# A two-layer graph kernel: node counts from the comparison instruction, and a new order of the head

## The chip, the cores and the metric

The kernel runs on one core of a Trainium2 chip. The metric is the device time of one execution in microseconds, given as the median over several runs. Every number below comes from those runs or from one profiled execution of the same kernel.

The engines are named as in the profile: PE is TensorE (PEld its loading of weights), DVE is VectorE, ACT is ScalarE, POOL is GpSimd. SP issues most of the DMA transfers, and its own entries carry a q (SPq).

## The reference

For each of N = 128 graphs there are C = 128 nodes with D = 512 features (x, fp32), and a 128 x 128 matrix adj of weights, many of them zero.

```python
H  = (adj != 0)                       # incidence: node c lies in hyperedge e
w  = adj[:, 0, :]                     # first row: the hyperedges' weights
Dn = 1 / sum_e H[c, e] * w[e]         # 0 where the sum is not positive
Be = 1 / sum_c H[c, e]                # one over the number of nodes of a hyperedge
hypergraph_conv(x, W, b) = Dn * (H @ (Be * (H.T @ (x @ W.T)))) + b

# layer 0
h = relu(layernorm(x))
r = layernorm(relu(hypergraph_conv(h, W1, b1))) * gamma + beta    # 512 -> 1024
x = x + h + hypergraph_conv(r, W2, b2)                            # 1024 -> 512
# layer 1
h   = relu(layernorm(x))
agg = (adj @ h) / max(sum_j adj[i, j], 1e-6)
x   = x + relu(concat(h, agg) @ W.T)                              # 1024 -> 512
```

All of it is fp32. W1, W2 and W are the same for all graphs.

## The kernel before

One graph fills the 128 partitions, so the work goes graph by graph. [...]each large product is made of three: both operands are split into a high part h and a low part l, with a third part d made from the two. `product` sums h x h and l x l in one PSUM bank ("main") and d x d in a second, four or eight 128x512 matmuls for each part. The weights are split once, in the head: `Half.high` (ScalarE), `Half.low` and `Half.rest` (VectorE), each on one half of a weight tile at a time (index 0 or 1). The activations are split per graph: `conv1_high/low/rest` (z), `inner_high/low/rest` (n), `layer1_high/low/rest` (h, "layer 1's first operand"), `layer1_mean_high/low/rest` (b). In the profile w10h is the high part of the first half of W1, w31d the third part of the second half of W (w3), and so on; rm and rd are the two banks of the first convolution's product, gm and gd of the second's, bm/bd and am/ad of layer 1's two.

The stages of a graph, with the tiles that the text speaks of:

- `load_adjb` and `load_adj` fetch adj, once in 32x32 blocks (four transfers, adjb) and once as it is; `load_x` fetches x.
- `x_sums`, `x_spread`, `scales`, `x_norm`: the layer norm of x. ScalarE makes the two sums, VectorE the scales (lines 234 and 235, tile st), ScalarE the result h (line 239).
- `incidence` (VectorE, lines 290 to 299): transposes adj, compares with zero, counts the nodes of each hyperedge (cnt), and makes sb, the incidence divided by the count, with a further column of weights.
- `node_matrix`: TensorE makes S = H Be H.T and the sums for Dn from sb in one fp32 matmul (ps_s, line 305); ScalarE copies it to s. `node_scale` (VectorE, lines 315 to 319) makes Dn out of it.
- `conv1_nodes`: S is applied to h ahead of W1 (pz, line 343). `conv1_weights`: the product with W1, in two halves. `conv1_main` (ScalarE), `conv1_out` and `conv1_bias` put together r.
- `inner_sums`, `inner_spread`, `inner_norm`, `inner_out`, `inner_in`, `inner_turn`: relu and layer norm of r, then a way through DRAM (n_scratch, then nb) and a 32x32 transpose (nt), since the next product needs r with its features on the partitions.
- `conv2_weights`, `conv2_main`, `conv2_weights_out`, `conv2_bias`, `conv2_nodes`, `conv2_out`: second convolution; S is applied behind the weights here (py, line 517). `residual` adds h and b2 to x (GpSimd).
- `layer1_*`: layer norm, the same way through DRAM (h_scratch, hb, ht), product with both halves of W. `mean_operator`, `mean_out`, `mean_in`, `mean_transpose` make adj divided by its row sums, transposed and split (anp). `aggregate` multiplies it into the second half's product, three matmuls, the third of which needs the part bd (line 475).

In the head `beta_row(k)` multiplies the raw W2 by beta on TensorE (pc, line 185), and `scale_w2(k)` then scales that block of W2 by gamma; only after it can the block be split.

The order on each engine is written out by hand: `tc.manual_schedule()` keeps the program's order, so an instruction stands in its engine's queue where the program calls it, and waits there for its inputs. `head()` is a list of stages for the first graphs; then `step(s)` runs for s from -4 to 126, each with stages of five graphs in one fixed order; then `tail()`. `stage` keeps a set of what was done, so a step leaves out what the head did already. DMA issues stand in SP's queue in the program's order too, and each uses one of eight semaphores in turn, so it also waits for the transfer issued eight before it.

Of the kernel before, what the change touches and what calls it, by code (L numbers as in the profile page):

```python
# [24 lines left out]
def gnn_kernel(  # L25
# [31 lines left out]
    nc = tc.nc  # L57
# [124 lines left out]
    def beta_row(k):  # L182
        if not BETA:
            BETA.append(bank("pc"))
        nc.tensor.matmul(BETA[0], vector_of(0, k).to_broadcast([P, P]), w2[k // KD].raw[:, k % KD],
                         start=(k == 0), stop=(k == KH - 1))
# [15 lines left out]
    @stage  # L202
    def load_x(g):
        X[g] = pool.tile([P, D], FP, tag="x", name="x_t", bufs=6)
        nc.sync.dma_start(out=X[g], in_=x[g])
# [6 lines left out]
    @stage  # L212
    def load_adjb(g, queue=nc.sync):
        ADJB[g] = pool.tile([P, P], FP, tag="adjb", name="adjb", bufs=2)
        load_blocks(ADJB[g], adj[g], queue)
# [15 lines left out]
    @stage  # L231
    def scales(g, kind):
        t = STATS[kind, g]
        nc.vector.reciprocal(t[:, 4:5], t[:, 3:4])  # L234
        nc.vector.tensor_tensor(t[:, 5:6], t[:, 1:2], t[:, 4:5], MUL)  # L235
# [49 lines left out]
    @stage  # L285
    def incidence(g):


        HT[g] = at = pool.tile([P, P], FP, tag="ht", name="adjt")
        nc.vector.transpose(at, ADJB.pop(g))  # L290
        SB[g] = sb = pool.tile([P, P + 1], FP, tag="sb", name="sb")
        nc.vector.tensor_scalar(sb[:, P : P + 1], at[:, 0:1], DOWN_12, None, MUL)
        nc.vector.tensor_scalar(at, at, 0.0, None, ALU.not_equal)
        cnt = pool.tile([P, 1], FP, tag="cnt", name="cnt", bufs=2)
        nc.vector.tensor_reduce(cnt, at, AX.X, ADD)

        nc.vector.tensor_scalar(cnt, cnt, 1.0, None, MAX)
        nc.vector.reciprocal(cnt, cnt)
        nc.vector.tensor_scalar(sb[:, :P], at, cnt, None, MUL)
# [26 lines left out]
    @stage  # L326
    def x_spread(g):
        spread((1, g), X[g], H0[g], D)

    @stage  # L330
    def x_norm(g):
        normalise((1, g), H0[g], X[g], AF.Relu)
# [63 lines left out]
    @stage  # L396
    def conv1_weights(g, half):
        PR[g, half] = product(Z[g], w1[half : half + 1], lambda pm: PY.update({(g, half): pm}), "r")

    @stage  # L400
    def conv1_main(g, half):
        if half == 0:
            R[g] = pool.tile([P, DH], FP, tag="r", name="r")
        copy(R[g][:, HALVES[half]], PY.pop((g, half)), AF.Copy, scale=DN[g][:, 1:2])  # L404
# [6 lines left out]
    @stage  # L411
    def conv1_bias(g, half, eng=nc.gpsimd):
        r = R[g][:, HALVES[half]]
        combine(eng, r, r, b1_bc[:, HALVES[half]], ADD)
# [268 lines left out]
    def head():  # L683
        copy(eps_root, eps, AF.Sqrt)
        load_x(0)
        load_adjb(2)
        for half in range(2):
            for i in range(2):
                load_w1(half, i)
        load_affine()  # L690
        load_adjb(0, nc.scalar)
        load_x(1)
        load_adjb(1)
        x_sums(0)
        load_adj(0)
        x_spread(0)
        for half in range(2):
            load_w2(half)
        load_bias(b2_bc, b2)
        w1[0].high(0)  # L700
        scales(0, 1)
        x_norm(0)
        w1[0].high(1)
        incidence(0)
        load_x(2)
        w1[0].low(0)
        node_matrix(0)
        conv1_nodes(0)
        w1[0].low(1)
        w1[1].high(0)  # L710
        w1[0].rest(0)
        conv1_high(0)
        w1[1].high(1)
        load_bias(b1_bc, b1)
        conv1_low(0)
        conv1_rest(0)
        incidence(1)
        x_sums(1, "A")
        x_spread(1)
        node_scale(0)  # L720
        w1[0].rest(1)
        scales(1, 1)
        w1[1].low(1)
        x_norm(1)
        conv1_weights(0, 0)
        beta_row(0)
        scale_w2(0, nc.scalar)
        conv1_main(0, 0)
        beta_row(1)
        scale_w2(1, nc.scalar)  # L730
        w1[1].low(0)
        w1[1].rest(0)
        w1[1].rest(1)
        node_matrix(1)
        node_scale(1)
        conv1_nodes(1)
        conv1_high(1, True)
        conv1_weights(0, 1)
        conv1_low(1)
        conv1_rest(1)  # L740
        beta_row(2)
        beta_row(3)
        conv1_main(0, 1)
        conv1_weights(1, 0)
        conv1_out(0, 0)
        scale_w2(2, nc.vector)
        scale_w2(3, nc.vector)
        conv1_bias(0, 0, nc.vector)
        w2[0].high(0)
        w2[0].high(1)  # L750
        conv1_out(0, 1)
        conv1_bias(0, 1, nc.vector)
        beta_row(4)
        beta_row(5)
        load_adjb(3)
        load_w3(0)
        load_w3(1)
        beta_row(6)
        beta_row(7)
        inner_sums(0)  # L760
        conv1_weights(1, 1)
        inner_spread(0)
        w2[0].low(1)
        residual(0)
        scale_w2(4, nc.vector)
        scale_w2(5, nc.vector)
        scales(0, 2)
        inner_norm(0)
        scale_w2(6, nc.vector)
        scale_w2(7, nc.vector)  # L770
        w2[0].low(0)
        incidence(2)
        inner_out(0)
        x_sums(2)
        x_spread(2)
        scales(2, 1)
        w2[1].high(0)
        w2[1].low(0)
        x_norm(2)
        node_matrix(2)  # L780
        w2[1].high(1)
        node_scale(2)
        load_adjb(4)
        conv1_nodes(2)
        conv1_main(1, 0)
        conv1_main(1, 1)
        conv1_high(2)
        w2[0].rest(1)
        conv1_low(2)
        conv1_rest(2)  # L790
        beta_out()
        inner_in(0)
        load_x(3)
        inner_turn(0)
        residual(1)
        conv1_out(1, 0)
        w3[0].high(0)
        conv1_bias(1, 0, nc.vector)
        w2[1].low(1)
        load_x(4)  # L800
        inner_high(0)
        conv1_weights(2, 0)
        conv1_out(1, 1)
        conv1_bias(1, 1, nc.vector)
        conv1_weights(2, 1)
        inner_low(0, nc.vector)
        w2[0].rest(0)
        inner_sums(1)
        inner_spread(1)
        w2[1].rest(0)  # L810
        scales(1, 2)
        inner_norm(1)
        inner_out(1)
        load_adjb(5)
        inner_rest(0)
        w3[0].high(1)
        w2[1].rest(1)
        incidence(3)
        conv2_weights(0)
        x_sums(3)  # L820
        x_spread(3)
        node_matrix(3)
        scales(3, 1)
        x_norm(3)
        residual(2)
        node_scale(3)
        conv2_main(0)
        conv1_main(2, 0)
        conv2_weights_out(0)
        conv1_nodes(3)  # L830
        conv2_bias(0, nc.vector)
        conv2_nodes(0)
        conv1_high(3, True)
        conv1_main(2, 1)
        conv1_low(3)
        conv1_rest(3)
        conv1_weights(3, 0)
        conv2_out(0)
        conv1_out(2, 0)
        conv1_bias(2, 0, nc.vector)  # L840
        layer1_sums(0)
        layer1_spread(0)
        inner_in(1)
        inner_turn(1)
        conv1_out(2, 1)
        conv1_bias(2, 1, nc.vector)
        inner_high(1)
        scales(0, 3)
        inner_low(1, nc.vector)
        inner_rest(1)  # L850
        layer1_norm(0)
        layer1_trip_out(0)
        w3[1].high(0)
        conv2_weights(1)
        inner_sums(2)
        inner_spread(2)
        w3[0].low(1)
        scales(2, 2)
        conv2_main(1)
        inner_norm(2)  # L860
        conv2_weights_out(1)
        mean_operator(0)
        conv2_bias(1, nc.vector)
        inner_out(2)
        conv2_nodes(1)
        conv1_weights(3, 1)
        w3[1].low(0)
        mean_out(0)
        w3[0].low(0)
        conv2_out(1)  # L870
        layer1_trip_in(0)
        w3[1].high(1)
        mean_in(0)
        load_adj(1)
        x_sums(4)
        residual(3)
        x_spread(4)
        scales(4, 1)
        x_norm(4)
        incidence(4)  # L880
        layer1_turn(0)
        w3[1].low(1)
        layer1_high(0)
        node_matrix(4)
        mean_transpose(0)
        node_scale(4)
        layer1_low(0, nc.vector)
        inner_in(2)
        w3[0].rest(1)
        w3[1].rest(1)  # L890
        w3[1].rest(0)
        w3[0].rest(0)
        load_x(5)
        layer1_rest(0)
        load_adjb(6)

    def tail():
# [182 lines left out]
```

## Time and profile before

| | |
|---|---|
| median of 5 runs | 2514.6 us (2514.28 to 2516.56) |
| the profiled execution | 2515.8 us, span 2514.0 us |
| mean granted TensorE clock | 0.994 |
| instructions in the profile | 41377 |
| PE busy in 260 to 1300 us | 1039.02 of 1040 us |

The span is the time from the first to the last instruction of the program. A line of the time line gives start, length, engine, source line, operation, output and inputs, the number of instructions merged into it, and in brackets the idle time of the engine ahead of it and what ended that. All starts are microseconds from the start of the span.

### The profile page before, as it was taken

Reading aid. Unit: us, or ns where it says so; the run is one execution under the profiler, and the core shown is the slowest. Engines: PE = TensorE matmul, PEld = TensorE weight load, DVE = VectorE, ACT = ScalarE, POOL = GpSimd, SP = SyncE. Lnnn points to the kernel's source line nnn. Section 1 sums busy time; section 2 is a strip of 40 time slices with the busy share of each in tenths; the row PEclk is TensorE's granted clock in tenths of the full one; section 3 lists DMA queues with packets and bytes.
Section 4 is the critical chain, followed back from the end, with each engine's and each line's share of the span. In section 5 each row is a group of like instructions: output and inputs, shape, how many; then the busy total and the mean of one; then the engine's idle time right before and its main releaser. Section 6 shows DMA issues by size and latency. Waiting matters only on the chain. (4 is left out here: it accounts for less than half of the span.)

```text
span 2514.0 us, 41377 instructions
## 1 busy us (share of the span) xinstructions
PE 2470.1 (98%) x11152; PEld 2004.4 (80%) x11152; DVE 2122.1 (84%) x4907; ACT 1977.7 (79%) x4112; POOL 1739.6 (69%) x2290
## 2 busy tenths in 40 slices
PE   6899999999999999999999999999999999999997
PEld 4688887888888888888888888888888888888885
DVE  7988888888888888888888888888888888888885
ACT  6787787778778878878887887887888788788874
POOL 2477677677767767777776776777677667767763
PEclk9899999999999999999999999999999999999999
DMA  6343344344344434333343443443444344344332
GB/s 175 95 127 121 125 126 122 122 127 128 119 126 127 125 121 133 120 123 126 124 125 126 127 121 122 130 126 120 125 127 125 120 133 121 120 128 129 120 120 83
DMA packets 409674, 311.90 MB, mean 124 GB/s; under 512 B 176736, under 2 KB 340576, under 8 KB 409440
## 3 DMA queue, kind: packets, MB, share of 16 engines
q1 hardware_dynamic: 408608, 309.18, 39.8%
q8 instruction: 88, 1.44, 0.2%
q14 instruction: 146, 1.20, 0.2%
q10 hardware_dynamic: 576, 0.07, 0.0%
q0 software_dynamic: 256, 0.01, 0.0%
HBM read 166.47 MB, written 142.61 MB: 123 GB/s over the span
## 5 line engine op out<-in xcount | busy, mean ns | idle before, releaser
L80 POOL TENSOR_TENSOR g<-g,c 128x256 f32<-128x256 f32 x252 | 181.4, 743 | 524.1 <-DVE g L508 400.4
L80 POOL TENSOR_TENSOR r<-r,b_bc 128x256 f32<-128x256 f32 x500 | 356.7, 744 | 20.6 <-DVE st L234 11.6
L80 POOL TENSOR_TENSOR nl<-nt,nh 128x256 fp32r<-128x256 f32 x504 | 358.2, 747 | 5.0 <-ACT nh L466 5.0
L80 POOL TENSOR_TENSOR hl<-ht,hh 128x256 fp32r<-128x256 f32 x254 | 180.9, 734 | 147.0 <-ACT hh L466 147.0
L80 POOL TENSOR_TENSOR x_t<-x_t,h 128x256 f32<-128x256 f32 x256 | 240.4, 962 | 47.0 <-ACT h L239 47.0
L80 POOL TENSOR_TENSOR bl<-gb_t,bh 128x256 fp32r<-128x256 f32 x256 | 260.2, 1040 | 9.7 <-PE am L385 9.7
L504 ACT ACTIVATE g<-gm 128x512 f32<-128x512 f32 x128 | 76.4, 597 | 212.9 <-PE gm L385 212.7
L239 ACT ACTIVATE h<-x_t,st 128x512 f32<-128x512 f32 x256 | 207.8, 812 | 35.2 <-DVE st L235 23.2
L475 DVE SCALAR_TENSOR_TENSOR nd<-nh,nl 128x1024 fp32r<-128x1024 f32 x128 | 208.1, 1626 | 25.2 <-POOL nl L80 25.2
L445 DVE STREAM_TRANSPOSE nt<-nb 128x1024 f32<-128x1024 f32 x128 | 159.4, 1245 | 61.1 <-DMA nb<-n_scratch 59.6
L223 ACT ACTIVATE h<-x_t 128x512 f32<-128x512 f32 x256 | 160.2, 626 | 60.7 <-DVE x_t L521 58.6
L80 POOL TENSOR_TENSOR x_t<-x_t,b_bc 128x256 f32<-128x256 f32 x256 | 184.8, 742 | 14.0 <-DMA b_bc<-in_b_dram 14.0
L385 PE MATMUL rm<-w11h,z 128*128 128x512 f32 x512 | 190.5, 494 | 0.0
L228 ACT ACTIVATE h<-x_t,st 128x512 f32<-128x512 f32 x256 | 184.7, 722 | 4.3
L409 DVE SCALAR_TENSOR_TENSOR r<-rd,dinv,r 128x512 f32<-128x512 f32 x256 | 186.3, 728 | 0.9 <-ACT r L404 0.6
L404 ACT ACTIVATE r<-rm,dinv 128x512 f32<-128x512 f32 x256 | 171.4, 670 | 3.1 <-DMA n_scratch<-r 1.4
L239 ACT ACTIVATE r<-r,st 128x1024 f32<-128x1024 f32 x128 | 158.0, 1234 | 1.7 <-DVE st L235 1.5
L385 PEld LDWEIGHTS rm<-w11h,z 128*128 128x128 f32 x512 | 96.6, 189 | 72.0 <-issue 60.2
L385 PE MATMUL bm<-w30h,hh 128*128 128x512 f32 x512 | 150.3, 415 | 3.3 <-ACT hh L466 3.3
L466 ACT ACTIVATE nh<-nt 128x1024 fp32r<-128x1024 f32 x128 | 135.2, 1056 | 19.3 <-DVE nt L445 18.6
L343 PEld LDWEIGHTS pz<-s,h 128*128 128x128 f32 x1024 | 134.3, 192 | 14.9 <-ACT s L307 4.0
L605 DVE SCALAR_TENSOR_TENSOR o<-ad,o 128x512 f32<-128x512 f32 x128 | 88.5, 692 | 68.1 <-ACT o L593 67.2
(127 smaller groups left out, 7251.7 us busy)
## 6 DMA issues: line engine op xcount, KB each, us to landing
n_scratch<-r SPq DMA_DIRECT2D x128, 512.0 KB, 2.6
nb<-n_scratch SPq DMA_DIRECT2D x512, 128.0 KB, 2.8
x_t<-in_x_dram SPq DMA_DIRECT2D x128, 256.0 KB, 2.8
h_scratch<-h SPq DMA_DIRECT2D x128, 256.0 KB, 2.1
hb<-h_scratch SPq DMA_DIRECT2D x512, 64.0 KB, 2.0
out_dram<-o SPq DMA_DIRECT2D x128, 256.0 KB, 2.8
adj_t<-in_adj_dram SPq DMA_DIRECT2D x128, 64.0 KB, 1.8
an_scratch<-adj_t SPq DMA_DIRECT2D x128, 64.0 KB, 2.6
```

The source lines that it names most:

```text
L80: eng.tensor_tensor(dst[:, s], a[:, s], b[:, s], op)
L223: copy(junk, src, func, accum_out=t[:, 0:1])
L228: copy(junk, src, AF.Square, bias=t[:, 1:2], accum_out=t[:, 2:3])
L239: copy(dst, src, func, bias=t[:, 5:6], scale=t[:, 4:5])
L343: nc.tensor.matmul(z[:, k * P : (k + 1) * P], H0[g][:, k * P : (k + 1) * P], S[g], start=True, stop=True)
L385: nc.tensor.matmul(pm, left[i](k), right(i, k), start=(i == 0 and k == 0), stop=(i == 1 and k == kk - 1))
L404: copy(R[g][:, HALVES[half]], PY.pop((g, half)), AF.Copy, scale=DN[g][:, 1:2])
L409: nc.vector.scalar_tensor_tensor(r, PR.pop((g, half)), dn[:, 0:1], r, MUL, ADD)
L445: nc.vector.transpose(nt.rearrange("p k (i b) -> p k i b", b=B), t.rearrange("p i k a -> p k i a"))
L466: copy(h, a, AF.Copy, scale=DOWN)
L475: nc.vector.scalar_tensor_tensor(t, h, 2.0**-12, low, MUL, SUB)
L605: nc.vector.scalar_tensor_tensor(o, pd, 4096.0, o, MUL, ADD)
```

## The change

Two things are changed. In `incidence`, which runs for each of the 128 graphs, the comparison with zero also sums its results along the row and writes the sum to cnt; the separate sum is gone. And in `head()` stages stand in another order; the stages themselves, `step` and `tail` are as before. In the last part of the head, layer 1's first operand for graph 0 (`layer1_low`, `layer1_rest`) is made ahead of the third parts of W's second half.

```diff
@@ incidence
-        nc.vector.tensor_scalar(at, at, 0.0, None, ALU.not_equal)
         cnt = pool.tile([P, 1], FP, tag="cnt", name="cnt", bufs=2)
-        nc.vector.tensor_reduce(cnt, at, AX.X, ADD)
+        nc.vector.tensor_scalar(at, at, 0.0, None, ALU.not_equal, ADD, accum_out=cnt)
@@ head
         load_adjb(0, nc.scalar)
+        load_adjb(1)
         load_x(1)
-        load_adjb(1)
         x_sums(0)
         load_adj(0)
         x_spread(0)
+        scales(0, 1)
...
         w1[0].high(0)
-        scales(0, 1)
+        load_x(2)
+        w1[0].high(1)
         x_norm(0)
-        w1[0].high(1)
         incidence(0)
-        load_x(2)
...
         conv1_rest(0)
-        incidence(1)
         x_sums(1, "A")
...
         w1[1].low(1)
         x_norm(1)
+        incidence(1)
         conv1_weights(0, 0)
+        conv1_main(0, 0)
         beta_row(0)
         scale_w2(0, nc.scalar)
-        conv1_main(0, 0)
+        node_matrix(1)
         beta_row(1)
+        w1[1].low(0)
         scale_w2(1, nc.scalar)
-        w1[1].low(0)
         w1[1].rest(0)
         w1[1].rest(1)
-        node_matrix(1)
-        node_scale(1)
         conv1_nodes(1)
...
         conv1_main(0, 1)
-        conv1_weights(1, 0)
+        w2[0].high(0)
         conv1_out(0, 0)
         scale_w2(2, nc.vector)
+        load_adjb(3)
         scale_w2(3, nc.vector)
+        conv1_weights(1, 0)
         conv1_bias(0, 0, nc.vector)
-        w2[0].high(0)
         w2[0].high(1)
         conv1_out(0, 1)
         conv1_bias(0, 1, nc.vector)
         beta_row(4)
+        load_w3(1)
+        load_w3(0)
         beta_row(5)
-        load_adjb(3)
-        load_w3(0)
-        load_w3(1)
         beta_row(6)
+        node_scale(1)
+        residual(0)
         beta_row(7)
         inner_sums(0)
         conv1_weights(1, 1)
+        w2[0].low(1)
         inner_spread(0)
-        w2[0].low(1)
-        residual(0)
         scale_w2(4, nc.vector)
         scale_w2(5, nc.vector)
         scales(0, 2)
-        inner_norm(0)
         scale_w2(6, nc.vector)
+        x_sums(2)
         scale_w2(7, nc.vector)
         w2[0].low(0)
         incidence(2)
+        inner_norm(0)
         inner_out(0)
-        x_sums(2)
         x_spread(2)
...
         w2[1].low(0)
+        node_matrix(2)
         x_norm(2)
-        node_matrix(2)
+        node_scale(2)
         w2[1].high(1)
-        node_scale(2)
...
         inner_in(0)
-        load_x(3)
         inner_turn(0)
         residual(1)
         conv1_out(1, 0)
         w3[0].high(0)
-        conv1_bias(1, 0, nc.vector)
+        load_x(3)
+        conv1_out(1, 1)
         w2[1].low(1)
         load_x(4)
+        conv1_bias(1, 0, nc.vector)
         inner_high(0)
         conv1_weights(2, 0)
-        conv1_out(1, 1)
         conv1_bias(1, 1, nc.vector)
...
-        load_adjb(5)
         inner_rest(0)
         w3[0].high(1)
+        load_adjb(5)
...
         conv1_high(3, True)
+        conv1_low(3)
         conv1_main(2, 1)
-        conv1_low(3)
...
         layer1_norm(0)
-        layer1_trip_out(0)
         w3[1].high(0)
         conv2_weights(1)
+        layer1_trip_out(0)
+        mean_operator(0)
         inner_sums(2)
...
         conv2_weights_out(1)
-        mean_operator(0)
         conv2_bias(1, nc.vector)
         inner_out(2)
+        mean_out(0)
+        w3[1].low(0)
         conv2_nodes(1)
+        w3[0].low(0)
         conv1_weights(3, 1)
-        w3[1].low(0)
-        mean_out(0)
-        w3[0].low(0)
-        conv2_out(1)
         layer1_trip_in(0)
         w3[1].high(1)
         mean_in(0)
         load_adj(1)
+        residual(3)
         x_sums(4)
-        residual(3)
...
         incidence(4)
+        conv2_out(1)
         layer1_turn(0)
...
         node_scale(4)
+        inner_in(2)
+        w3[0].rest(0)
         layer1_low(0, nc.vector)
-        inner_in(2)
         w3[0].rest(1)
+        layer1_rest(0)
+        w3[1].rest(0)
         w3[1].rest(1)
-        w3[1].rest(0)
-        w3[0].rest(0)
         load_x(5)
-        layer1_rest(0)
         load_adjb(6)
```

## The prediction

> **What bounds the kernel now.** I read the page first, then busy time by stretches, then the time line of the first 100 us engine by engine, last the DMA landings.
>
> ```profile
> PE 2470.1 (98%) x11152; PEld 2004.4 (80%) x11152; DVE 2122.1 (84%) x4907; ACT 1977.7 (79%) x4112; POOL 1739.6 (69%) x2290
> ```
> ```profile
> 0.00:20.00 20.00, 8.09 (x23) 5.90 (x24) 11.52 (x30) 11.36 (x22) 6.09 (x14) 1.00 0.77 217
> ...
> 60.00:80.00 20.00, 16.69 (x52) 11.73 (x52) 17.09 (x32) 14.36 (x28) 2.52 (x4) 0.76 0.23 77
> 80.00:100.00 20.00, 15.37 (x59) 11.88 (x58) 19.26 (x38) 11.71 (x27) 11.75 (x14) 0.81 0.23 65
> 100.00:120.00 20.00, 20.00 (x92) 16.34 (x92) 17.83 (x42) 16.23 (x33) 13.11 (x18) 1.00 0.43 130
> ...
> 1300.00:2350.00 1050.00, 1049.84 (x4789) 856.72 (x4788) 900.35 (x2092) 844.16 (x1766) 756.00 (x992) 1.00 0.40 125
> ```
>
> The first line is busy time by engine; the others give start and length of a stretch, busy us of TensorE, weight loads, VectorE, ScalarE and GpSimd, then the granted clock, DMA share and GB/s. From 100 us on TensorE is never idle (1049.84 of 1050), at the full clock, 19.07 us per graph. There a faster VectorE is worth nothing. All of TensorE's loss lies in the first 95 us (some 27 us idle, and a lower clock in four places) and in the last 64, which the change doesn't touch. So the change is worth what it moves the moment from which TensorE runs without a pause. These lines carry the head:
>
> ```profile
> 10.62 0.80 PE L305 MATMUL ps_s<-sb,adjt 128*128 128x129 f32 x2 [10.62 <-DVE sb L299]
> ...
> 23.18 1.16 PE L343 MATMUL pz<-s,h 128*128 128x128 f32 x8 [1.09 <-ACT s L307]
> ...
> 38.92 0.49 PE L305 MATMUL ps_s<-sb,adjt 128*128 128x129 f32 x2 [1.18 <-DVE sb L299]
> ...
> 54.78 1.20 PE L389 MATMUL gd<-w20d,nd 128*128 128x512 f32 x4 [0.86 <-DVE nd L475]
> ...
> 75.94 1.10 PE L517 MATMUL py<-g,s 128*128 128x512 f32 x2 [2.43 <-DVE g L80]
> ...
> 89.48 2.07 PE L389 MATMUL bd<-w30d,hd 128*128 128x512 f32 x4 [3.93 <-DVE hd L475]
> ```
> ```profile
> 8.80 0.23 DVE L293 TENSOR_SCALAR adjt<-adjt 128x128 f32<-128x128 f32 x1
> 9.06 0.29 DVE L295 TENSOR_REDUCE cnt<-adjt 128x1 f32<-128x128 f32 x1
> ...
> 34.87 0.17 DVE L234 RECIPROCAL st<-st 128x1 f32<-128x1 f32 x1 [1.08 <-ACT st L229]
> ...
> 73.60 0.69 DVE L508 TENSOR_TENSOR g<-gd,g 128x512 f32<-128x512 f32 x1 [0.29 <-PE gd L389]
> 74.21 0.27 DVE L249 TENSOR_REDUCE deg<-adj_t 128x1 f32<-128x128 f32 x1
> ...
> 85.34 2.35 DVE L136 TENSOR_TENSOR w31d<-w31l,w31h 128x1024 fp32r<-128x1024 f32 x2
> 87.61 1.21 DVE L136 TENSOR_TENSOR w30d<-w30l,w30h 128x1024 fp32r<-128x1024 f32 x1
> 88.75 0.68 DVE L475 SCALAR_TENSOR_TENSOR hd<-hh,hl 128x512 fp32r<-128x512 f32 x1
> ...
> 100.57 0.69 DVE L475 SCALAR_TENSOR_TENSOR bd<-bh,bl 128x512 fp32r<-128x512 f32 x1
> ```
>
> Each bracket is idle time and what ended it. VectorE is the late one. Three things are to be seen: g waits at 74.21 behind four mean_operator instructions; hd waits behind the weights' parts w31d; and at 34.87 VectorE itself waits for ScalarE's statistics.
>
> **The comparison.** Removed per graph: comparison and sum, 0.58 us from start to start (8.80 to 9.38). In their place is one comparison that also sums. No row shows that form. The nearest rows: the sum alone 0.286 us; ScalarE's separate accumulator read, 0.19 busy, about 0.22 from start to start; a 128x1 VectorE operation, 0.18 from start to start. Ends: a free sum at the comparison's own 0.26 saves 0.32; 0.32 + 0.22 = 0.54 saves 0.04, and 0.1 more than that would lose 0.06. Against the change speaks the Trainium skill, "SBUF — State Buffer", section "Who interferes with whom": a tensor_scalar that writes out its accumulator can't enter the two-port mode. By that the comparison loses its 0.227 and costs about the sum's 0.286; with a read of 0.18 behind it I take 0.45, a saving of about 0.15 (by the two-port row it would be 0.2). In the stream, 120-odd times 0.15 us is hidden behind TensorE: nothing. Only the graphs of the head count.
>
> **0 to 28 us.** w10h's second part goes ahead of the first norm. Its weights land at 9.28 (issued 4.50, 4.8 in flight), so ScalarE runs it 9.33 to 10.3, the norm to 11.1, and copies s at 11.0 to 11.28 (11.46 to 11.74 before). sb is ready earlier than that, as GpSimd's first addition (9.76) no longer runs beside it: L299 took 0.80 there, 0.29 otherwise. pz at 11.35 instead of 11.79: 0.44 gained.
> On SP's queue the four adjb transfers of graph 1 now stand ahead of x of graph 1. The first waits for the transpose (8.6), so x is issued at about 11.0, not 5.97. What is in flight lasts anyway until w11r at 13.65; x lands near 15.7, not 14.54. Its sum began at 15.34: ScalarE, with everything queued behind it, is 0.4 late there. Later weights move by tenths.
> incidence(1), 1.7 us, leaves its place ahead of w10d's second half (which TensorE waited 0.24 for) and comes after w11l's first: sb(1) at about 20.9. TensorE: first product at 14.1, beta_row(0) 19.4 to 20.3 (w20r is there at 19.36), 0.6 idle, ps_s at 20.9, beta_row(1) 21.15 to 22.0. Under that beta row ScalarE copies s, so pz starts at 22.0 and not 23.18: **1.2 gained**.
>
> **28 to 55 us.** The bias of r ends 1.2 earlier, as does ScalarE's statistics of r. node_scale(1), 0.7 us, is put in here; the 1.08 idle at 34.87 takes it. x_sums(2), 1.05 us, ahead of inner_norm(0) fills ScalarE's wait for scales, and puts n_scratch at 35.8 instead of 36.54; nb then lands near 43.4, when VectorE asks for it. incidence(2) ends some 1.35 earlier, s and the norm bring rm to 41.6 (42.99), and VectorE runs without a pause to nd: gd at 53.45 instead of 54.78, **1.3 gained**. The other moves here swap neighbours inside one full stretch: nothing; a wait for nb would show as a delay of a few tenths.
>
> **Moves costed at nothing.** conv1_main(0, 0) ahead of the first scale_w2 runs in ScalarE's wait for the beta row (0.56 at 21.05). load_x(2), load_x(3), load_adjb(3), load_adjb(5), mean_out and layer1_trip_out keep their order on SP. residual(0) and residual(3) keep theirs on GpSimd, and residual(0) waits for b2 till 25.0 anyway. conv1_out(1, 1) ahead of w21l makes that 0.74 later, still 3.5 us before its product. conv1_low(3) ahead of conv1_main(2, 1) is on another engine's queue. w31d after hd is ready at about 87.1, its product comes 0.5 to 3 us later, by the clock. If VectorE were not full there, each would cost at most its own 0.7 to 1.2.
>
> **55 to 76 us.** ScalarE's norm sets pz(3), so the faster incidence gives nothing. mean_operator(0), 0.90 us (74.21 to 75.11), goes from between g and its bias to before w30l, where VectorE idled 1.18. py(1) at 73.75: 1.3 + 0.9 = **2.2 gained**.
>
> **76 to 95 us.** VectorE is full. conv2_out(1) goes behind incidence(4): the same sum. hd no longer stands behind two w31d parts (2.27), so bd comes at 89.48 - 2.2 - 0.15 - 2.27 = about 84.9. hl stands behind one w30d part more, which costs bm's second block 1.1 inside that wait. But nl of the next product is GpSimd's (93.34 to 96.17), behind a bias that waits for r, and r moves only with VectorE's sum: 2.2 + 0.15, less 0.15 for statistics. nl ends at 93.95, gm's third block had 1.16 us to spare (97.33): 3.4 gained there. At the aggregate's third matmul (101.63) VectorE's bd ends at 101.26; it gains 2.2 + 2 x 0.15 = 2.5, plus 0.37 to spare: **2.9 gained**. That is the last clamp: after it TensorE waits for nobody. SP's order is unchanged there but for w31 before w30, both landed 6 us ahead of use.
>
> The sum is 2.9 us. The profiled execution took 2515.8 (span 2514.0, 1.8 around it), so it would be 2512.9; the shown runs' median is 1.2 below it: 2514.6 - 2.9 = **2511.7 us**.
>
> **The clock, weighed.** TensorE's granted clock halves in the stretches 43.2 to 46.6, 60.2 to 67.1, 77.3 to 80.7 and 87.5 to 94.4, all on one grid of 3.41 us; it fell after grid windows with 1.8 to 2.1 us idle, not after one with 1.5. The Trainium skill, "TensorE: Matmul & The Clock Gate", "What's actually happening", says that it falls after an idle window of 3.4 us and that windows run free. By the rule only the 3.93 gap would slow anything, and a shorter one would pay 1 to 2 us more than my sum; by the trace half a window is enough. I follow the trace: bd's slow stretch is hidden by nl's clamp, the one at 77 by VectorE. Only 60.2 to 67.1 counts (5.8 us of work at half speed, 2.9 lost), and its gaps (0.71 + 1.07 + 0.88) stay in sum.
>
> **Rivals.**
> A, more than 0.2% faster: gaps fall otherwise on the grid, the slow stretch at 60 stays away or is half as long. 1.5 to 2.9 more: 2508.8 to 2510.2; with a free sum and nl's clamp looser by 0.5, 2508. For it: the two clusters of the shown runs (2514.3 to 2514.6, 2516.3 to 2516.6), as a free grid would make. Against: those runs are in the median already.
> B, slower: the summing comparison costs more than it replaces. Its place is VectorE's stretch before bd, with 0.28 us to spare at 120.71 in every graph. Up to 0.58 + 0.28 = 0.86 us nothing happens; at 1.0 us, 0.14 x 120 = 17 us minus 2.9: 2529. Against: no 128x128 row free of waiting is over 0.31, and 0.92 us of VectorE's waits per graph could give way.
> C, x of graph 1 lands after 17: everything behind ScalarE's queue slips by 1.2, the head's first gain is lost: 2513. Or the change does nothing, for TensorE's waits only change their cause: 2514.6.
>
> **How the numbers follow.** My sum 0.52, A 0.28, C and no change 0.12, B or another per-graph stall 0.08. The sum's own range: 2510 to 2513.5 (0.5 each for comparison, nb and clock). The range 2507.6 to 2514.8 leaves out B and the ends of A and C. 0.2% is 5.0 us, about what a measurement of this kernel can tell from no change. My sum and C lie within it. Faster by over 0.2% (below 2509.6): 0.3, A and the sum's lower end. Slower: 0.08. Within: 0.62.
>
> **What would show it.** In the profile after: pz(1) without its 1.09 wait, VectorE's 1.08 wait shrunk to 0.3 or so, py(1) waiting 1.5 and not 2.43, bd 2 us or less in place of 3.93, a new wait of gm for nl; gd near 53.45, and TensorE unbroken from about 98. Wrong if comparison and read take over 0.6 us, if x's sum starts after 16.5, or if TensorE is idle anywhere between 110 and 2440.

## The result, and the profile after

| | before | after |
|---|---|---|
| median | 2514.85 us (2511.59 to 2518.41, 43 runs) | 2509.82 us (2508.8 to 2511.42, 25 runs) |
| ratio after / before | | 0.9981, 95% interval 0.9975 to 0.9986 |
| the profiled execution | 2515.8 us, span 2514.0 | 2510.83 us, span 2509.0 |
| mean granted clock | 0.994 | 0.996 |

By the ratio the change is worth 4.8 us (3.5 to 6.3), where 2.9 were forecast. First the changed kernel's busy time by engine, and two of the stretches (start and length, busy us of TensorE, weight loads, VectorE, ScalarE and GpSimd, clock, DMA share, GB/s):

```profile
PE 2467.5 (98%) x11152; PEld 2000.6 (80%) x11152; DVE 2091.2 (83%) x4907; ACT 1978.5 (79%) x4112; POOL 1741.5 (69%) x2290
```
```profile
80.00:100.00 20.00, 16.42 (x68) 11.12 (x69) 19.30 (x40) 13.81 (x30) 9.76 (x13) 1.00 0.28 91
...
1300.00:2350.00 1050.00, 1049.91 (x4789) 856.64 (x4789) 884.50 (x2091) 843.52 (x1762) 750.91 (x991) 1.00 0.40 125
```

VectorE lost 31 us in all (2122.1 to 2091.2), 16 of them in the stretch from 1300 to 2350, where TensorE was full in both kernels. From 80 to 100 the clock is now full, where it was 0.81. The time line of TensorE in the head:

```profile
19.12 1.10 PE L185 MATMUL pc<-w20r,gb 128*128 128x512 f32 x2 [0.50 <-DMA w20r<-in_w2t_dram]
...
21.20 1.16 PE L342 MATMUL pz<-s,h 128*128 128x128 f32 x8
...
52.80 1.19 PE L388 MATMUL gd<-w20d,nd 128*128 128x512 f32 x4 [0.68 <-DVE nd L474]
...
73.09 1.10 PE L516 MATMUL py<-g,s 128*128 128x512 f32 x2 [1.66 <-DVE g L80]
...
84.40 1.19 PE L388 MATMUL bd<-w30d,hd 128*128 128x512 f32 x4 [0.54 <-DVE hd L474]
...
89.57 1.21 PE L384 MATMUL gm<-w20h,nh 128*128 128x512 f32 x4 [1.25 <-ACT nh L465]
...
95.18 1.19 PE L388 MATMUL gd<-w20d,nd 128*128 128x512 f32 x4 [1.04 <-DVE nd L474]
...
98.24 0.50 PE L598 MATMUL ad<-bd,anp 128*128 128x512 f32 x1
```

pz(1) no longer waits (1.09 before); it now follows a 0.50 wait for the weights w20r. bd waits 0.54 and not 3.93. New are the waits of gm for ScalarE's nh and of gd for VectorE's nd. The last line is the aggregate's third matmul of graph 0, at 101.63 before; between 97.2 and 2440 us TensorE is idle for 0.21 us in all (before: 1.14 between 105 and 2440). VectorE's time line shows the comparison and the last part of the head:

```profile
8.41 0.29 DVE L294 TENSOR_SCALAR_CACHE_REDUCE adjt<-adjt 128x128 f32<-128x128 f32 x1
8.62 0.08 DVE L294 DVE_READ_ACCUMULATOR adjt<-adjt 128x1 f32 x1
8.74 0.15 DVE L296 TENSOR_SCALAR cnt<-cnt 128x1 f32<-128x1 f32 x1
...
33.21 0.16 DVE L234 RECIPROCAL st<-st 128x1 f32<-128x1 f32 x1 [0.48 <-ACT st L229]
...
82.52 1.22 DVE L136 TENSOR_TENSOR w30d<-w30l,w30h 128x1024 fp32r<-128x1024 f32 x1
83.66 0.68 DVE L474 SCALAR_TENSOR_TENSOR hd<-hh,hl 128x512 fp32r<-128x512 f32 x1
...
97.50 0.69 DVE L474 SCALAR_TENSOR_TENSOR bd<-bh,bl 128x512 fp32r<-128x512 f32 x1
```

The new form is two instructions, 0.33 us from start to start (8.41 to 8.74) where comparison and sum took 0.58. hd stands right behind one w30d part. The last line is the bd that the aggregate's third matmul needs: it ends at 98.19, 0.05 us ahead of it.

### The profile page after: what moved, and what is told of

The parts are those of the page before. It is cut to its first block, busy times and chain, and to the rows that moved or that the text cites. A ratio compares the mean times of both kernels' runs of the same rounds, so it can differ in the third digit from the quotient of the medians.

```text
span 2509.0 us, 41379 instructions
## 1 busy us (share of the span) xinstructions
PE 2467.5 (98%) x11152; PEld 2000.6 (80%) x11152; DVE 2091.2 (83%) x4907; ACT 1978.5 (79%) x4112; POOL 1741.5 (69%) x2290
## 4 chain that ended last, share of the span: by engine, by line
PE 92%; POOL 2%; issue 2%; DVE 1%; DMA 1%; ACT 1%; SPq 1%; POOLq 0%; DVEq 0%; ACTq 0%
PE rm L384 18%; PE gm L384 17%; PE bm L384 9%; PE rd L388 9%; PE am L384 9%; PE gd L388 9%; PE bd L388 4%; PE pz L342 4%; PE ad L388 4%; PE py L516 4%; PE am L598 2%; PE ad L598 1%; PE ps_s L304 1%; POOL nl L80 0%; POOL bl L80 0%
## 5 line engine op out<-in xcount | busy, mean ns | idle before, releaser
L223 ACT ACTIVATE h<-x_t 128x512 f32<-128x512 f32 x256 | 160.2, 626 | 62.2 <-DVE x_t L520 60.2
L384 PEld LDWEIGHTS rm<-w11h,z 128*128 128x128 f32 x512 | 96.5, 189 | 72.0 <-issue 60.2
```

The source lines that it names most:

```text
L223: copy(junk, src, func, accum_out=t[:, 0:1])
L384: nc.tensor.matmul(pm, left[i](k), right(i, k), start=(i == 0 and k == 0), stop=(i == 1 and k == kk - 1))
```

## The experiments

Two marks are read from each profile: the start of the aggregate's third matmul of graph 0 (`ad<-bd`; "the head"), and the time from there to the same matmul of graph 123, less 123 x 19.05 us ("the stream"). A profile is one execution; the ratio is of many runs, each kernel against before on the same chip.

| kernel | ratio to before, 95% | in us | head | stream | head + stream against before's two |
|---|---|---|---|---|---|
| before; again | 1; 0.9998 (0.9989 to 1.0007) | 0; -0.5 | 101.63; 102.07 | 3.94; 2.34 | 0 |
| after | 0.9981 (0.9975 to 0.9986) | -4.8 | 98.24 | 3.21 | -3.5 |
| after again | 0.9984 (0.9977 to 0.9990) | -4.0 | 98.93 | 1.88 | -4.2 |
| count only | 0.9992 (0.9984 to 1.0001) | -2.0 | 101.37 | 1.90 | -1.7 |
| order only | 0.9996 (0.9988 to 1.0005) | -1.0 | 99.02 | 5.01 | -1.0 |
| order only again | 0.9996 (0.9987 to 1.0005) | -1.0 | 99.66 | 3.55 | -1.8 |
| old start | 0.9988 (0.9981 to 0.9994) | -3.0 | 100.87 | 2.02 | -2.1 |
| old end of head | 0.9984 (0.9977 to 0.9990) | -4.0 | 100.70 | 1.88 | -2.4 |
| mean_operator back | 0.9984 (0.9977 to 0.9991) | -4.0 | 98.78 | 1.97 | -4.2 |
| scale on ScalarE | 0.9987 (0.9980 to 0.9993) | -3.3 | 99.50 | 2.60 | -2.9 |
| one more sum | 1.0002 (0.9993 to 1.0011) | +0.5 | 100.03 | 4.76 | -0.2 |
| two more sums | 1.0063 (1.0050 to 1.0075) | +15.8 | 100.88 | 19.04 | +14.9 |
| w30d on GpSimd | 1.0003 (0.9994 to 1.0012) | +0.8 | 103.88 | 2.24 | +1.1 |

"In us" is the ratio less 1, times 2515. The last column takes 104.99, the mean of before's two sums, from each kernel's own. The two agree within 1.6 us everywhere, and the intervals' half-widths are 1.4 to 3.1 us. From the last mark to the end of the span it is 64.2 to 65.6 us in all profiles, in no order that fits the changes. So head and stream together hold most of the effect, and a difference under 2 us between two kernels' times settles nothing alone.

**The count alone, and the order alone.** `incidence` as changed with before's head:

```diff
-        nc.vector.tensor_scalar(at, at, 0.0, None, ALU.not_equal)
-        nc.vector.tensor_reduce(cnt, at, AX.X, ADD)
+        nc.vector.tensor_scalar(at, at, 0.0, None, ALU.not_equal, ADD, accum_out=cnt)
```

> The old head with the summing comparison alone. Theory of the record: TensorE waits for nobody in the stream, so the 0.25 us that each graph saves on VectorE (0.58 to 0.33 from start to start) counts in the head alone: 0.2 to 0.5 us less than before, within the noise. Rival (slack): VectorE runs close behind TensorE in every graph, and now and then a late trip through DRAM pushes it over; 0.25 us more room per graph takes such stalls away. Then 1 to 2 us less than before, TensorE's idle time between 105 and 2440 us falls from 1.1 to 0.3 or less, and the runs lie closer together than before's.

The other is the changed kernel with before's two lines in `incidence`, the same edit turned round; it was run twice.

> The new head with the old comparison and sum. Theory of the record: all of the gain is the head's: 4.5 us or more less than before. Rival (slack): the head alone gives 2.5 to 3.3 us (in the trace after, the aggregate of graph 0 comes 3.4 earlier, of which incidence's own part is some 0.5), and the rest is missing: 2.5 to 3.5 us less than before, with stalls of up to 1 us left in the stream.

> The new order of the head with the old comparison and sum, a second time. If its stream of 5.0 us over 123 x 19.05 belongs to it (TensorE, put ahead by the head, leaves VectorE less room, and the old comparison cannot make it up): again 4 to 6, aggregate of graph 0 at about 99, time 2513 to 2514.5. If it was that one execution: 2 to 4, and a time of 2511 to 2512.5.

The count alone left the head nearly where it was (101.37). Its time is 2.0 us less, but the interval still holds no change; its stream is 1.90, and before's two are 3.94 and 2.34. So the rival's 1 to 2 us fits, but the 0.2 to 0.5 of the theory of the record is not excluded: with the old head a gain in the stream isn't shown. The order alone brought the head to 99.02 and 99.66, 2.5 earlier on the mean, but only 1.0 us in the time, which is less than either expectation (2.5 to 3.5, or 4.5 and more); its stream was 5.01 and 3.55. So of the 2.5 that the new order gains by the profiles about 1.1 was lost again behind it (4.3 on the mean, before's two 3.1), and by the time somewhat more, while the comparison was the old one. With the new head the comparison is therefore worth 3.4 us by the ratios (4.4 for after's two on the mean, 1.0 here; the intervals of order only meet after again's at their ends alone, and after's not at all) and 2.8 by the profiles: 0.8 in the head, 2.0 in the stream. The second profile's 3.55 lies in the band that was written for "one execution", its time in the other's; the pair still lies above every stream measured with the summing comparison at the new head (1.88 to 3.21).

**The whole change again, and before again.** No edit.

> The kernel after once more, for a second profile and times on the same chip as the three above. Both theories: 4 to 5.5 us less than before. It tells how far the head's marks (pz of graph 1 at 21.2, gd at 52.8, py of graph 1 at 73.1, the aggregate of graph 0 at 98.2) move from one execution to the next: by under 0.3 if the head is set by the program alone, by 1 to 2 if by the clock's grid and the landings.

> The kernel before, a second time. If the old comparison costs the stream about 2 us: 3 to 5 us over 123 x 19.05, the aggregate of graph 0 at 101 to 102.5, time 2514 to 2515. If the first profile's late graph at 386 us was chance: 2 to 2.6 over, with the same head.

after again: head 98.93, stream 1.88. From after's first profile to its second pz(1) moved by 1.15 us, gd by 1.61, py(1) by 0.72 and the aggregate by 0.69, so the head isn't set by the program alone. before again: head 102.07, stream 2.34, as was expected if the first profile's late graph was chance: that profile was at the high end of its stream (the late graph told of below is not in the second). Two against two the head is 3.3 us earlier and the stream 0.6 shorter.

**Undoing one part of the order.** Old start: `head()` in before's order up to conv1_nodes(1), and node_scale(1) with it (cut to the lines that set pz(1)):

```diff
         conv1_rest(0)
+        incidence(1)
         x_sums(1, "A")
...
         x_norm(1)
-        incidence(1)
         conv1_weights(0, 0)
...
         beta_row(1)
...
         w1[1].rest(1)
+        node_matrix(1)
+        node_scale(1)
         conv1_nodes(1)
```

Old end: the last part in before's order,

```diff
         layer1_low(0, nc.vector)
+        inner_in(2)
         w3[0].rest(1)
-        layer1_rest(0)
-        w3[1].rest(0)
         w3[1].rest(1)
+        w3[1].rest(0)
+        w3[0].rest(0)
         load_x(5)
+        layer1_rest(0)
```

with inner_in(2) and w3[0].rest(0) gone from ahead of it. And mean_operator(0) back between g and its bias, as before:

```diff
         layer1_trip_out(0)
-        mean_operator(0)
         inner_sums(2)
...
         conv2_weights_out(1)
+        mean_operator(0)
         conv2_bias(1, nc.vector)
```

> The kernel after with the head's first part (up to conv1_nodes(1)) in the order before. Theory of the record: 1.2 to 1.3 us of the head's gain goes (pz of graph 1 waits for s again, about 1.1; gd comes 1.3 later), so about 3.5 less than before and 1.3 lost against after. Rival: the start is set by when weights land and on which grid of the clock, and the profile's 1.98 at pz is mostly that: 0.5 or less lost.

> The kernel after, with layer 1's first operand of graph 0 again behind the last weights' third parts (end of the head as before). Theory of the record: hd and bd come 2.3 us later (86.7 instead of 84.4), but nl and nd clamp the next product at the same place, so only 0 to 1 us is lost against after: 3.8 to 4.8 less than before; 0.9 lost only if the slow clock returns there. Rival: the wait for hd was TensorE's largest (3.93), its removal is the gain: 2.2 us lost against after, 2.6 less than before.

> The kernel after, with mean_operator(0) again between g and its bias. Theory of the record: py(1) 0.9 us later (74.0 instead of 73.1) and all of VectorE behind it: 0.9 lost against after, about 3.9 less than before. Rival: VectorE's stretch behind it has room now (0.34 us of waiting at 75.56, 1.0 at gd), so 0.3 or less is lost.

One line of TensorE's time line each, of the old end and of mean_operator back:

```profile
88.35 2.08 PE L388 MATMUL bd<-w30d,hd 128*128 128x512 f32 x4 [3.78 <-DVE hd L474]
```
```profile
74.03 1.10 PE L516 MATMUL py<-g,s 128*128 128x512 f32 x2 [2.43 <-DVE g L80]
```

Each undone part brings its wait back. With the old start pz(1) waits 0.76 for s and is at 24.76, and the head is 2.3 later than after's mean of 98.6. That is more than the part is worth, as this pz(1) is 1.6 later even than before's 23.18; all profiles together put it at 1.7 (see below).

With the old end bd comes 13.53 after py(1), as before (13.54) and not 11.31. The head is 2.1 later than after's mean, but 1.4 of it was there already at py(1) (74.82; 73.09 and 73.81 in after's two). From py(1) to the aggregate it takes 25.88 us, and 25.15 and 25.12 in after's two. So this part moves bd by 2.2 us and the head by 0.7.

With mean_operator back, py(1) waits 2.43. It is 0.94 later than in after's first profile, whose gd stands at the same place (52.80; 52.89 here); bd is 0.52 later and the head 0.54. So some 0.4 us of it was made up, and against after again (bd 85.07, head 98.93) nothing is seen of it. The times of these three lie within 1 us of after again's and decide none of the expectations: the parts are told apart by their places in the profile.

**What VectorE's time in the stream is worth.** One more sum per graph,

```diff
         nc.vector.tensor_scalar(at, at, 0.0, None, ALU.not_equal, ADD, accum_out=cnt)
+        nc.vector.tensor_reduce(cnt, at, AX.X, ADD)
```

two more (the same line twice), and the other way, the product of line 235 taken from VectorE to ScalarE:

```diff
-        nc.vector.tensor_tensor(t[:, 5:6], t[:, 1:2], t[:, 4:5], MUL)
+        copy(t[:, 5:6], t[:, 1:2], AF.Copy, scale=t[:, 4:5])
```

> The changed kernel with one more sum over a row for every graph, about 0.32 us of VectorE: comparison and sums then take 0.65 us a graph, a little more than the 0.58 of before. The slack theory (VectorE's room in the stream is thin, and each tenth more costs some more late graphs): from the aggregate of graph 0 to that of graph 123, 4 to 7 us over 123 x 19.05 where the changed kernel has 1.9 to 3.2 and before 3.9; the time is 2 to 4 us above the changed kernel's, 2512 to 2514. The theory of the record (up to 0.86 us nothing happens): the stream as in the changed kernel, and 0 to 0.5 us more, 2509.8 to 2511, from the head's few graphs alone.

> The kernel after with two more sums of the same row in incidence, each 0.32 us from start to start, whose result is the count again: VectorE has 0.64 us less room per graph than after, 0.39 less than before. Theory of the record (TensorE has room in the stream): 0 to 1 us lost against after, all of it in the head. Slack theory: a late trip pushes TensorE further and in more graphs; the time that graphs 0 to 123 take over 19.05 us each, 1.9 to 3.2 us with the summing comparison and 3.9 to 5.0 with comparison and sum, grows to 7 or more: 4 us or more lost, slower than the head alone.

> The kernel after, with the product of mean and scale in the three layer norms (VectorE, line 235, 0.34 us on average, three per graph) moved to ScalarE just ahead of the norm: about 0.6 us from start to start less per graph on VectorE, 0.7 more on ScalarE, which has 20% idle. Theory of the record: no gain in the stream; in the head each norm comes 0.1 later: 0 to 1 us slower than after. Slack theory: graphs 0 to 123 fall to 1.5 us or less over 19.05 us each, 0.5 to 1.5 us faster than after, and the runs lie closer together.

The sum costs what it cost in before (0.32 from start to start), so at the new head the four prices of comparison and sums are 0.33, 0.58, 0.65 and 0.97 us, and the streams 2.3 (mean of after, after again, mean_operator back and w30d on GpSimd), 4.3 (mean of two), 4.8 and 19.0. About 2.0 of each is an even pace: the median graph takes 19.06 to 19.07 us in every profile but that of two more sums (19.155). The rest is in late graphs. One more sum undid the whole gain: 1.0002 against 0.9981, with intervals that don't meet. Its stream and that of two more sums are as the slack theory had them (4 to 7, and 7 or more).

Most of what is lost is lost at one place, the aggregate's third matmul, which needs VectorE's bd. Its spare is the time from the end of bd to the start of that matmul. What is lost there is read from the start of the matmul ahead of it to the start of the one behind it, above the median of 0.46 us (graphs 1 to 123):

| kernel | median spare of bd, us | graphs with under 0.15 | lost there, us |
|---|---|---|---|
| before; again | 0.54; 0.74 | 4; 5 | 1.1; 0.8 |
| count only | 0.91 | 6 | 0.7 |
| after; again | 0.75; 0.98 | 4; 3 | 1.0; 0.6 |
| order only; again | 0.54; 0.61 | 12; 8 | 2.3; 1.4 |
| one more sum | 0.60 | 10 | 2.2 |
| two more sums | 0.38 | 47 | 11.2 |
| scale on ScalarE | 1.11 | 0 | 0 |

The four profiles left out have 2 to 4 such graphs and lost 0.4 to 0.7 us.

Little of it shows as idle time of TensorE (3.29 us at all places together in the stream of two more sums), since the record of such a matmul lasts 0.39 us where the next one starts 0.23 behind it: a wait shorter than the difference leaves no gap. VectorE is late there where data came late to it. All profiles but that of two more sums have 64 graphs with under 0.15 us of spare. In these VectorE had waited 1.9 us for DMA in the 15 us ahead of the matmul (median), in all their other graphs 0.9. Where VectorE is later still, gd waits for nd as well, as here with two more sums:

```profile
2171.92 1.19 PE L390 MATMUL gd<-w20d,nd 128*128 128x512 f32 x4 [0.67 <-DVE nd L476]
```

The product on ScalarE freed VectorE of 56 us between 1300 and 2350, one per graph, and bought nothing in the time (its stretch, the columns as above):

```profile
1300.00:2350.00 1050.00, 1050.00 (x4794) 857.61 (x4792) 828.26 (x1927) 884.83 (x1927) 753.61 (x990) 1.00 0.40 125
```

No bd was late any more, yet the stream was 2.60 and the time no better than after's, where the slack theory had 0.5 to 1.5 us less. So the first quarter microsecond mattered and this further one did not: gd waited for nd in some graphs (once 0.40), and ScalarE is 41 us fuller here, which may have cost some of it.

**A version meant to beat both.** The two w30d parts made by GpSimd, idle from 60 to 76 in after:

```diff
         w3[0].low(0)
+        w3[0].rest(0, nc.gpsimd)
+        w3[0].rest(1, nc.gpsimd)
...
         inner_in(2)
-        w3[0].rest(0)
         layer1_low(0, nc.vector)
-        w3[0].rest(1)
         layer1_rest(0)
```

> The changed kernel, with the third parts w30d of W's second half made by GpSimd instead of VectorE. Theory of the head (between py(1) and bd VectorE is full, so what is taken off it there comes off TensorE's end): VectorE is freed of 2.3 us there, bd comes about 2 us after py(1) earlier (11.3 us in the changed kernel, 9 to 10 here), but of that ScalarE's and VectorE's parts n give back up to 1 us, so the aggregate starts 1.0 to 2.2 us earlier and the time is 2508 to 2509.5. Rival (the last clamp is not VectorE's work but n's parts and the aggregate's own bd): the aggregate starts within 0.4 us of the changed kernel's and the time is the same. Third: GpSimd's two instructions slow VectorE's beside them or come later than their product needs, and bd comes later: 2511 to 2513.

All three expectations missed: it is 5.5 us slower than after. The third had the direction, parts that come later than they are needed, but not the amount and not the reason. GpSimd's, ScalarE's and TensorE's time lines of it:

```profile
75.11 4.67 POOL L136 TENSOR_TENSOR w30d<-w30l,w30h 128x1024 fp32r<-128x1024 f32 x2 [32.57 <-issue]
```
```profile
81.17 0.63 ACT L223 ACTIVATE h<-x_t 128x512 f32<-128x512 f32 x1 [7.93 <-POOL x_t L80]
```
```profile
85.47 0.80 PE L304 MATMUL ps_s<-sb,adjt 128*128 128x129 f32 x2 [8.79 <-DVE sb L298]
```

In after GpSimd was idle there because it had run ahead: its next work, residual(3), stands behind w3[0].low(0) in the program and ran at 57.17. Put ahead of it, the two parts wait for w30l till 75.11, residual(3) waits behind them till 79.73, ScalarE's next sums (line 223) wait 7.93 us for it, and TensorE 8.79. The same parts behind residual(3) were not tried; whether less work on VectorE there is worth anything stays open.

## Why the prediction was right, and where it was not

The median, 2509.82 us, lies in the stated range (2507.6 to 2514.8), but not where the sum had it: it is below the sum's own range (2510 to 2513.5) and in the one given for rival A (2508.8 to 2510.2), for a reason that A doesn't name. The head gave about what the sum had for it. The rest came in the stream, which had been put at nothing. That a range drawn wide for A covered it is luck.

**Right: the head's chain, and its sum.** 2.9 us were forecast for it, and the two profiles of after have 3.3 on the mean against the two of before. Point by point:

- *Start.* pz(1) lost its 1.09 wait as told. The gain was 2.0 in the profile and 1.7 over all profiles (old start 22.60 to 24.76, mean 23.4; new 21.15 to 22.35, mean 21.7), not 1.2. The term that was too dear is x of graph 1: put at 15.7, it landed at 14.29, since w11r, which it followed, landed at 12.73 and not at 13.65; its sum ran at 14.86 and delayed nothing. What was late next was w20r, 0.50.
- *28 to 55.* VectorE's wait at 34.87 shrank to 0.48 (0.3 forecast). gd came at 52.80, 31.60 after pz(1) as before: all of its gain is the start's, as forecast within 0.2.
- *55 to 76.* 0.9 forecast for mean_operator; gd to py(1) fell from 21.16 to 20.29, and is 21.14 with it put back. The wait was 1.66 (1.5 forecast).
- *76 to 95.* 2.27 forecast for the parts behind hd: py(1) to bd fell from 13.54 to 11.31.
- *The clamp behind it.* Of the sum at bd (4.6) 1.7 was to be given back. It was 1.5: from bd to the aggregate 12.5 us with the old end (before twice, count only, old end), 14.0 with the new (after twice, order only twice). But the engine named was wrong: no wait for GpSimd's nl came, gm waited for ScalarE's nh and gd for VectorE's nd. All three hang on VectorE's r and nt (86.53 and 87.19), which move only with VectorE's sum. That this holds was right; which part of n comes last was not. The last clamp is the one that the sum ends on: bd of VectorE, which had 0.37 us to spare in before, ends 0.05 ahead of the matmul in after. It came 3.1 earlier and not 2.5, mainly by the start's surplus.

**Wrong: the stream.** The step that failed reads "There a faster VectorE is worth nothing", and in the comparison's part "In the stream, 120-odd times 0.15 us is hidden behind TensorE: nothing". It went by the sum of busy time (1049.84 of 1050), and by 0.28 us to spare at 120.71, taken to hold in every graph. The place was the right one, but the graphs are not alike: in before the spare there is 0.54 at the median and under 0.28 in 23 of 123 graphs (19 in before again). These are VectorE's and TensorE's lines of before ahead of the mark of graph 15:

```profile
377.38 1.25 DVE L445 STREAM_TRANSPOSE nt<-nb 128x1024 f32<-128x1024 f32 x1 [2.63 <-DMA nb<-n_scratch]
```
```profile
386.11 1.20 PE L389 MATMUL gd<-w20d,nd 128*128 128x512 f32 x4 [0.93 <-DVE nd L475]
```

and of after ahead of the same mark:

```profile
373.45 1.25 DVE L444 STREAM_TRANSPOSE nt<-nb 128x1024 f32<-128x1024 f32 x1 [1.95 <-DMA nb<-n_scratch]
...
383.81 0.68 DVE L474 SCALAR_TENSOR_TENSOR bd<-bh,bl 128x512 fp32r<-128x512 f32 x1
```
```profile
384.11 0.40 PE L598 MATMUL am<-bl,anp 128*128 128x512 f32 x1
384.55 0.50 PE L598 MATMUL ad<-bd,anp 128*128 128x512 f32 x1
```

Beside it the graph that is on time, of before, at 120.71:

```profile
120.48 0.39 PE L599 MATMUL am<-bl,anp 128*128 128x512 f32 x1
120.71 0.40 PE L599 MATMUL ad<-bd,anp 128*128 128x512 f32 x1
```

In both kernels VectorE gets nb late and must catch up. In before gd missed by 0.93, and from mark to mark it took 20.62 us. In after gd came in time, but bd ended at 384.49, the aggregate's third matmul came 0.44 and not 0.23 behind the one ahead of it, and the graph took 19.33 us. The two differ by more than the comparison, as VectorE waited 0.7 us longer for nb in before. A late bd costs up to 0.3 us and shows no idle time, so a busy sum over a thousand us can't show it; room on VectorE is what absorbs it. The DMA view of before shows the write that was late, and the queues beside it, first between 364 and 379, then a graph earlier (345 to 360):

```profile
q8 instruction: 1, 0.02, 0.4%
...
n_scratch<-r SPq DMA_DIRECT2D x1, 512.0 KB, 4.5
```
```profile
n_scratch<-r SPq DMA_DIRECT2D x1, 512.0 KB, 2.6
```

Beside the late one (4.5 us) a 16 KB packet of an instruction queue is under way, which the earlier stretch has not. Over all fourteen profiles, 466 of the 1699 such writes issued between 100 and 2420 us meet a packet of an instruction queue: median 2.85 us, up to 4.50, and 174 of them over 3.0. Of the other 1233 none took over 2.80. That they belong together is seen in these counts, it was not tried. Nor is it all: of the 64 graphs with a late bd counted above, the write of 32 met no such packet.

How much the stream gave is known only within bounds: 0.6 two against two, 2.0 for the comparison at the new head (4.3 against 2.3). Why the old comparison's stream is worse with the new order (4.3) than with the old (3.1) is open; bd was late in more graphs there (12 and 8, against 4 and 5).

**Mis-sized: the comparison.** 0.15 us saved was taken, between 0.04 and 0.32; it is 0.25. The instruction's own view, of 128 executions:

```profile
L294 DVE TENSOR_SCALAR_CACHE_REDUCE adjt<-adjt x128: 285/286/289, 8.4 to 2423.2; 128x128 f32<-128x128 f32 x128
L294 DVE DVE_READ_ACCUMULATOR adjt<-adjt x128: 82/83/85, 8.6 to 2423.4; 128x1 f32 x128
```

The rule that was weighed fits: the comparison takes the sum's 286 ns and not the 227 that it took without the sum (the Trainium skill, "SBUF — State Buffer", section "Who interferes with whom": this form can't enter the two-port mode). The read was sized by ScalarE's (0.19) and a small VectorE operation (0.18 from start to start); from its start to the next instruction it is 0.12, and it begins 0.21 after the comparison.

**The clock.** The stretch at 60 stayed, 6.8 us long as forecast (58.4 to 65.2); those at 77 and 87 are gone. That the one at 87 was hidden is borne out by the old end, which brings it back (86.8 to 93.7) and still has the aggregate only 0.7 later behind py(1). Rival A's form (a stretch that stays away) showed in after again, where none fell at 60 and gd to py(1) took 19.40 and not 20.3. But its stretch at 41 was 6.8 us long and not 3.4, and its head came no earlier: the slow stretches fall differently from one execution to the next.

**The rivals.** B's direction was right: with two more sums (0.97 us) the time is 21 us above after's, where its form, 0.11 x 120, gives 13. But its threshold of 0.86 is none: at 0.65 the gain was gone already. It named the place rightly and took the spare to be the same in every graph. C did not come, as x landed early.

## What to carry to other kernels

A stretch in which the engine that sets the time is 99.98% busy (1049.84 of 1050) can still stand in a run that late rounds made longer. Look at the rounds one by one for the late ones, by the times from start to start and not by idle time alone; find the instruction that waits there, and how much spare its input has at the median and in the worst rounds. A quarter of a microsecond for each of 120 rounds paid through the few that came late, and a further one, bought with ScalarE's time, paid nothing. An engine's idle stretch is not free room where its queue is in program order: before putting work there, find what stands behind it and who waits for that.

## What the runs showed of the hardware

- **The clock falls after half an idle window, and comes back only after a nearly full one.** Over the windows of 3.41 us in the heads of these profiles, the clock halved after every window with TensorE idle for 1.75 us or more (and after two, with 1.59 and 1.64), and stayed full after others with up to 1.69 (before: fell after 1.78, stayed after 1.51; after: fell after 2.09 and 1.77, stayed after 1.62). Once low it came back at the end of a window with 0 to 0.48 us idle and stayed low through one with 0.57 or more: that is why a slow stretch is 3.4 us long (before's 43.2 to 46.6, no idle in it) or 6.8 (60.2 to 67.1, 0.88 in its first window). The Trainium skill, "TensorE: Matmul & The Clock Gate", "What's actually happening", has the window's length and that it runs free, and so it is here; its "idle window" is here one that is idle by half.
- **Packets of an instruction queue go with late transfers:** without one beside it no 512 KB write to DRAM took over 2.80 us (1233 writes in fourteen profiles), with one they took up to 4.50 (466 writes, median 2.85). That the one causes the other was not tried.
- **Reading VectorE's accumulator is cheap:** 83 ns, and 0.12 us from its start to the next instruction's; ScalarE's takes 0.19 us.
